# Reordering one DMA queue in every second step of an attention loop: two halves of a move around a send, and a fetch behind them

## The chip, the cores and the metric

The kernel runs on one core of one Trainium2 chip. The metric is device time in microseconds (us) of one execution. The kernel before took 906.04 us as the median of three runs (905.31 to 906.72 us). Everything is in 32-bit floating point.

## The reference

Two layers work on `x` of 16 x 256 x 256 (4096 tokens of 256 channels). Each does `x = x + s * silu(f)`, with `s` and `f` computed from a layer norm of `x`. In layer 0, `s` is a linear recurrence and `f` a two-layer perceptron. Layer 1, where the change is, has causal attention with 16 heads for `s` and a base projection with a routed low-rank part for `f`:

```python
q = (x @ Wq).reshape(B, S, N_HEADS, QK_DIM)                     # 128 plain + 64 rotated
q = jnp.concatenate([q_nope, apply_rope(q_rope)], axis=-1)
k = jnp.concatenate([k_nope, jnp.broadcast_to(k_rope, ...)], axis=-1)
scores = jnp.einsum('bqhd,bkhd->bhqk', q, k) * scale            # causal mask, S = 256
attn = jax.nn.softmax(scores, axis=-1)
out = jnp.einsum('bhqk,bkhd->bqhd', attn, v).reshape(B, S, N_HEADS * V_DIM) @ Wo
```

## The kernel before, in words

Layer 1 works through 8 chunks of 512 tokens (two batch rows of 256). In each chunk the 16 heads form 4 **groups** of 4 heads, so there are 32 groups, numbered n = 0 to 31. Each group takes two **slots** of the loop at L1653, one for each batch row b: slot i = 2n is the even slot of group n (b = 0), slot 2n + 1 its odd slot (b = 1). The whole order is written out by hand: each engine, and the DMA queue of SP (`sp`), is wrapped in `InOrder` (L45), which keeps its instructions in the order in which the loop calls them. The 64 slots run from about 266 us to 880 us of the span.

What one group needs, in order of time:

- `query_mm`, `query_mul`, `query_rot` (L389 to L428): TensorE projects the queries into `pq`; VectorE multiplies by the rotation tables; GpSimd forms the rotated queries `qrot` in two halves, r = 0 and then r = 1, each by one instruction. `qrot` has one buffer.
- `query_move` (L430): the queries must lie in other partitions, so eight DMAs of 64 KB on SP's queue copy `qrot` into the tile `qg`, first four (one for each head) for r = 0, then four for r = 1. Below, **R0** and **R1** are these two sets of four. This is done in the even slot of the group before.
- `score_pack` (L1369): TensorE multiplies `qg` with the keys into `sc`; VectorE adds the mask and takes the row maxima; ScalarE takes the exponential into `pr`; GpSimd normalises (`normalise`, L1405).
- `turn` (L1418): VectorE transposes `pr` in 32 x 32 blocks into `turned`, by three instructions in the slot after the scores.
- `send` (L1430): four DMAs of 192 KB write `turned` to a scratch tile `far` in DRAM. The **S0** send (b = 0) is issued in the group's own odd slot, the **S1** send (b = 1) in the even slot of the next group.
- `fetch` (L1444): four DMAs of 384 KB read `far` back into the tiles `pT`. F(y,b) fetches half y of batch row b: F(0,0) and F(1,0) in the even slot of the next group, F(0,1) and F(1,1) in the odd slot after that. Each waits until the sends of its b have landed.
- `values_of` (L1490): two slots after S1, in the even slot of group n + 2, TensorE multiplies `pT` with the values (`av`). It takes y = 0 first, b = 0 before b = 1, then y = 1.

So SP's queue issues 20 DMAs for each pair of slots. Before the change their order is

- even slot: R0 and R1 of group n + 1, F(0,0) of group n - 1, S1 of group n - 1, F(1,0) of group n - 1;
- odd slot: F(0,1) and F(1,1) of group n - 1, S0 of group n.

In the program as built, the DMAs of SP take eight completion semaphores in turn, and each waits for the landing of the one eight places ahead of it; at most eight are under way. SP waits in order: while one DMA waits, nothing behind it in the queue is issued.

Of the kernel before, what the change touches and what calls it, by code (L numbers as in the profile page):

```python
# [41 lines left out]
def tile_two_layers(ctx: ExitStack, tc: tile.TileContext, d: dict, out: bass.AP):  # L42
# [384 lines left out]
        gp.tensor_tensor(q.rot[:, 0, :], m0[:, 0, :], m1_[:, 1, :], ALU.subtract)  # L427
        gp.tensor_tensor(q.rot[:, 1, :], m1_[:, 0, :], m0[:, 1, :], ALU.add)  # L428

    def query_move(n):  # L430
        q = groups[n]
        for r in range(2):
            for h in range(G):
                sp.dma_start(
                    q.qg[64 + 32 * r : 96 + 32 * r, :, h, :],
                    q.rot[32 * h : 32 * h + 32, r, :].rearrange("p (a q) -> p a q", q=32),
                )


    with ExitStack() as l0:  # L440
# [177 lines left out]
        for k in range(8):  # L618
            n = 1 << k
# [714 lines left out]
    def gate_end(ch, jp):  # L1334
        k = chunks[ch]
        g = k.g2[:, 2 * jp : 2 * jp + 2, :]
        ve.scalar_tensor_tensor(g, g, 1.0, k.h, ALU.add, ALU.mult)
# [31 lines left out]
    def score_pack(u, pi):  # L1369
        k, b, pack = chunks[u.ch], u.b, PACK[pi]  # L1370
        if pi == 0:
            u.nm = sm1.tile([P, NQ], F32, tag="nm", name=f"nm_{u.n}", bufs=3)
            u.sr = sm1.tile([P, NQ], F32, tag="sr", name=f"sr_{u.n}", bufs=3)
        qg = groups[u.i // 2].qg
        sc = ps_sc.tile([P, CH], F32, tag="sc", name=f"sc_{u.n}_{pi}")
        halves = 2 if pi == 2 and u.b == 0 and u.i > 4 else 1
        m = P // halves
        for a, o in pack:
            w = qg[:, b * NQ + a, :, :].rearrange("p h q -> p (h q)")
            for y in range(halves):  # L1380
                pe.matmul(
                    sc[m * y : m * y + m, o : o + 32 * (a + 1)], w[:, m * y : m * y + m],
                    k.kT[:, b * S : b * S + 32 * (a + 1)], start=True, stop=True,
                )
        ends = [o + 32 * (a + 1) for a, o in pack]
        step = ends[1] - ends[0]
        n = len(pack)
        assert ends == [ends[0] + step * z for z in range(n)]
        if ends[0] - 32 + step * n <= CH:
            diag = sc[:, ends[0] - 32 : ends[0] - 32 + step * n].rearrange("p (n s) -> p n s", n=n)[:, :, 0:32]  # L1390
        else:
            diag = sc[:, ends[0] - step : ends[-1]].rearrange("p (n s) -> p n s", n=n)[:, :, step - 32 : step]
        ve.tensor_tensor(diag, diag, bc(kmask, n), ALU.add)
        for a, o in pack:
            ve.tensor_reduce(
                u.nm[:, a : a + 1], sc[:, o : o + 32 * (a + 1)], AX.X, ALU.max, negate=True
            )
        for a, o in pack:
            w = 32 * (a + 1)
            ac.activation(  # L1400
                u.pr[:, OFF[a] : OFF[a] + w], sc[:, o : o + w], AF.Exp,
                bias=u.nm[:, a : a + 1], accum_out=u.sr[:, a : a + 1],
            )

    def normalise(u, packs):  # L1405
        blocks = [a for pi in packs for a, _ in PACK[pi]]
        lo, hi = min(blocks), max(blocks) + 1
        ve.reciprocal(u.sr[:, lo:hi], u.sr[:, lo:hi])
        for a in blocks:
            v = u.pr[:, OFF[a] : OFF[a] + 32 * (a + 1)]  # L1410
            gp.tensor_scalar(v, v, u.sr[:, a : a + 1], 1.0, ALU.mult, ALU.mult)
# [32 lines left out]
    def fetch(n, y, b):  # L1444

        q = groups[n]
        if y == b == 0:
            q.pT = {}
        if b == 0:
            q.pT[y] = pp.tile([P, G, 3 * P], F32, tag="pT", name=f"pT_{n}_{y}", bufs=3)  # L1450
        sp.dma_start(
            q.pT[y][64 * b : 64 * b + 64].rearrange("p h q -> p (h q)"),
            q.far[b].rearrange("(y k) s h z q -> y (k s) (h z q)", y=2)[y],
        )
# [82 lines left out]
    def out_weights(i):  # L1537
        if i == PER:
            gp.tensor_tensor(TO[1], wo(0, 1), wo(0, 0), ALU.subtract)
            gp.tensor_tensor(TO[2], wo(1, 1), TO[1], ALU.subtract)  # L1540
        elif i == PER + 2:
            gp.tensor_tensor(TO[4], TO[2], wo(1, 0), ALU.subtract)
        elif i == PER + 4:
            gp.tensor_tensor(TO[3], wo(1, 1), wo(0, 1), ALU.subtract)
        elif i == 2 * PER + 1:
            TO[4] = X[0].rearrange("p j (n s) -> p (j n) s", s=DH)[:, 0:KP]
            gp.tensor_tensor(TO[4], TO[2], wo(1, 0), ALU.subtract)
# [45 lines left out]
    def fast_begin(ch, r):  # L1593

        k = chunks[ch]
        if r == 4:
            fast_sum(ch, (1, 1), (0, 1), (1, 1), ALU.add)
            fast_sum(ch, (0, 1), (0, 0), (0, 1), ALU.subtract)
        elif r == 5:
            fast_sum(ch, (0, 0), (1, 1), (0, 0), ALU.subtract)  # L1600
            fast_out(ch, 0, k.c00, (0,))
        elif r == 6:
            fast_sum(ch, (1, 0), (1, 0), (0, 0), ALU.subtract)
            k.c1 = a2.tile([P, 2, D], F32, tag="h", name=f"c1_{ch}", bufs=1)
            gp.tensor_tensor(k.c1[:, :, 0:DH], k.v, k.p4, ALU.subtract)
            gp.tensor_tensor(k.c1[:, :, DH:D], k.v, k.p5, ALU.add)
            gp.tensor_tensor(k.u, k.u, k.p5, ALU.add)
        elif r == 7:
            fast_out(ch, 1, k.c1, (0, 1))
            fast_store(ch, 1)  # L1610
        elif r == 0:
            fast_out(ch, 0, k.c01, (1,))
            fast_store(ch, 0)
# [39 lines left out]
    for i in range(LAST):  # L1653
        ch, r = divmod(i, PER)
        odd = i % 2 == 1
        u, w = units[i], units[i - 1] if i else None
        here = w is not None and w.i >= LAST - 2
        n = (i + 3) // 2 if odd else (i + 2) // 2
        n = n if n < len(groups) else None
        more = ch + 1 < NCH  # L1660
        last = ch - 1 if ch == NCH - 1 and r in FINISH else None
        fast = ch - 1 if 0 < ch < NCH - 1 else None

        if not odd and n is not None:
            query_move(n)
        if odd and i > 2:
            fetch((i - 3) // 2, 0, 1)
            fetch((i - 3) // 2, 1, 1)
        elif i and not odd:
            fetch((i - 2) // 2, 0, 0)  # L1670
        score_pack(u, 0)
        if w:
            normalise(w, (2,))
        if fast is not None and r > 3:
            fast_begin(fast, r)
        if ch > 1 and r == 0:
            fast_begin(ch - 2, 0)
        out_weights(i)
        if r == 1:
            gate_end(ch, 0)  # L1680
        if r == 2:
            gate_end(ch, 1)
            if more and ch:
                norm_end(ch + 1)
        if r == 5 and more:
            kv_end(ch + 1)
        if i == LAST - 1:

            finish_mm(last, 3, 0, NPAIR)
            finish_out(last, 3)  # L1690
            last = None
        if w:
            for z in (1, 2):
                turn_here(w, z) if here else turn(w, z)

        if r == 0:
            mid_chunk(ch)
        if r == 7 and more:
            key_chunk(ch + 1)
        if n is not None:  # L1700
            query_mm(n, 0 if odd else 3)
            if not odd:
                query_lat(n, 3)
        if i == 5:
            values_of(0)
        score_pack(u, 1)

        if odd and n is not None:
            query_mm(n, 1)
            query_mul(n, 0)  # L1710
        if w:
            if here:
                turn_here(w, 0)
            else:
                turn(w, 0)
                send(w)
        if not odd:
            if i > 4:
                values_of((i - 4) // 2)
            if i:  # L1720
                fetch((i - 2) // 2, 1, 0)
        score_pack(u, 2)
        normalise(u, (0, 1))

        if odd and n is not None:
            query_mm(n, 2)
            query_mul(n, 1)
            query_rot(n)
            query_lat(n, 2)
        if r < 2:  # L1730
            gate_begin(ch, r)
        if r == 0 and more and ch:
            norm_begin(ch + 1)
        if r == 2 and more:
            transpose_chunk(ch + 1)
        if r == 4 and more:
            kv_begin(ch + 1)
        if r == 6 and more:
            router_chunk(ch + 1)
        if last is not None:  # L1740
            j = FINISH.index(r)
            finish_mm(last, j, 0, NPAIR)
            finish_out(last, j)
        if fast is not None and r in FINISH:
            fast_end(fast, r)
# [94 lines left out]
```

## Time and profile before

| | |
|---|---|
| median of the runs | 906.04 us |
| profiled execution, its own time | 903.67 us |
| span of the profiled execution | 901.9 us |
| granted TensorE clock, mean | 0.994 |
| TensorE busy (PE) | 889.3 us, 99% of the span |
| VectorE, ScalarE, GpSimd busy | 667.4, 476.0, 571.2 us |
| DMA queue of SP | 128.69 MB, 58.0% of the span of 16 engines |
| from 300 to 857 us | PE busy 553.93 of 557.00 us, DMA share 0.81 |

The profiled execution took 1.77 us more than its span, and 2.37 us less than the median of the runs. In the profile's lines the file line of nearly all instructions is that of the wrapper, L53, so groups are told apart by their tiles: `far<-turned` is a send, `pT<-far` a fetch, `qg<-qrot` a move, `av<-pT,rowv` the matmuls of `values_of`. "SPq" is SP's queue; the duration of one of its rows runs from the first to the last issue that it merges. A fetch takes 4.0, 4.9 and 6.3 us from issue to landing (least, median, most), a send 2.3, 4.4 and 6.6 us, a move 2.1, 2.7 and 5.9 us.

### The profile page before, as it was taken

Reading aid. Unit: us, or ns where it says so; the run is one execution under the profiler, and the core shown is the slowest. Engines: PE = TensorE matmul, PEld = TensorE weight load, DVE = VectorE, ACT = ScalarE, POOL = GpSimd, SP = SyncE. Lnnn points to the kernel's source line nnn. Section 1 sums busy time; section 2 is a strip of 40 time slices with the busy share of each in tenths; the row PEclk is TensorE's granted clock in tenths of the full one; section 3 lists DMA queues with packets and bytes.
Section 4 is the critical chain, followed back from the end, with each engine's and each line's share of the span. In section 5 each row is a group of like instructions: output and inputs, shape, how many; then the busy total and the mean of one; then the engine's idle time right before and its main releaser. Section 6 shows DMA issues by size and latency. Waiting matters only on the chain.

```text
span 901.9 us, 17976 instructions
## 1 busy us (share of the span) xinstructions
PE 889.3 (99%) x5688; PEld 666.8 (74%) x5688; DVE 667.4 (74%) x2017; ACT 476.0 (53%) x1562; POOL 571.2 (63%) x885
## 2 busy tenths in 40 slices
PE   9999999999999989999999999999999999999988
PEld 8777999987757657776776777677677767766766
DVE  6886678764687869678868867886886788687642
ACT  3234665644436646655655565565556556556441
POOL 2229687787355537787586677758667775876531
PEclk9999999999999999999999999999999999999989
DMA  9730000000024888887887887788788768878880
GB/s 276 245 118 1 1 2 1 1 1 1 1 32 79 230 209 198 186 207 161 217 218 169 206 181 201 180 217 214 170 200 211 190 170 209 210 176 194 209 223 29
DMA packets 197406, 134.04 MB, mean 149 GB/s; under 512 B 143104, under 2 KB 187968, under 8 KB 197312
## 3 DMA queue, kind: packets, MB, share of 16 engines
q1 hardware_dynamic: 195184, 128.69, 58.0%
q0 software_dynamic: 1152, 3.67, 1.2%
q8 instruction: 46, 0.75, 0.4%
q10 hardware_dynamic: 976, 0.53, 0.2%
q14 instruction: 48, 0.39, 0.1%
HBM read 63.11 MB, written 52.95 MB: 129 GB/s over the span
## 4 chain that ended last, share of the span: by engine, by line
PE 93%; DVE 3%; DMA 2%; POOL 1%; ACT 1%; SPq 0%; issue 0%; ACTq 0%; POOLq 0%
PE pq L53 23%; PE sc L53 14%; PE po L53 11%; PE av L53 8%; PE f L53 7%; PE r L53 7%; PE pg L53 5%; PE ph L53 5%; PE pf L53 5%; PE pm L53 2%; PE pkv L53 2%; PE tp L53 2%; DMA far<-turned 1%; DMA pT<-far 1%; PE pb L53 1%; PE py L53 1%
## 5 line engine op out<-in xcount | busy, mean ns | idle before, releaser
L53 POOL TENSOR_SCALAR pr<-pr,sr 128x256 f32<-128x256 f32 (+7 forms) x512 | 192.5, 397 | 188.2 <-DVE sr L53 180.3
L53 ACT ACTIVATE pr<-sc,nm 128x256 f32<-128x256 f32 (+7 forms) x512 | 190.2, 382 | 217.1 <-DVE sr L53 139.6
L53 PEld LDWEIGHTS sc<-kT,qg 128*128 128x128 f32 (+1 forms) x1198 | 150.8, 176 | 54.8 <-issue 41.6
L53 PE MATMUL sc<-kT,qg 128*128 128x32 f32 (+6 forms) x1198 | 169.0, 290 | 0.0
L53 DVE TENSOR_REDUCE nm<-sc 128x1 f32<-128x256 f32 (+7 forms) x512 | 127.5, 301 | 6.6
L53 DVE STREAM_TRANSPOSE turned<-pr 128x512 f32<-128x512 f32 x186 | 123.2, 687 | 11.0 <-POOL pr L53 10.9
L53 PE MATMUL pq<-xnT,wlat 128*128 128x512 f32 x256 | 122.7, 602 | 0.0
L53 PE MATMUL pq<-xnT,wrope 128*128 128x512 f32 x256 | 120.2, 593 | 0.0
L53 ACT ACTIVATION_READ_ACCUMULATOR pr<-sc,nm 128x1 f32 x512 | 104.0, 203 | 0.0
L53 PE MATMUL av<-pT,rowv 64*64 64x512 f32 (+2 forms) x992 | 80.5, 445 | 6.0 <-DMA pT<-far 6.0
L53 POOL TENSOR_TENSOR qrot<-qmul,qmul 128x512 f32<-128x512 f32 x64 | 83.6, 1329 | 2.8 <-DVE qmul L53 2.8
L53 DVE TENSOR_TENSOR sc<-sc,kmask 128x96 f32<-128x96 f32 (+1 forms) x192 | 45.2, 236 | 53.8 <-PE sc L53 52.5
L53 DVE TENSOR_TENSOR qmul<-pq,rot_q 128x512 f32<-128x512 f32 x128 | 80.7, 672 | 0.1
L53 ACT ACTIVATE qg<-pq 64x512 f32<-64x512 f32 x128 | 75.5, 590 | 4.3 <-PE pq L53 3.5
L53 PEld LDWEIGHTS av<-pT,rowv 64*64 64x64 f32 x992 | 39.8, 135 | 43.6 <-issue 30.1
L53 PEld LDWEIGHTS pq<-xnT,wrope 128*128 128x128 f32 x256 | 45.7, 191 | 32.4 <-issue 32.1
L53 PEld LDWEIGHTS pq<-xnT,wlat 128*128 128x128 f32 x256 | 45.7, 191 | 31.6 <-issue 31.6
L53 PEld LDWEIGHTS po<-wout,attT 128*128 128x128 f32 x416 | 59.3, 193 | 9.8 <-issue 3.5
L53 PE MATMUL po<-wout,attT 128*128 128x128 f32 (+1 forms) x416 | 65.3, 311 | 0.0
L53 POOL TENSOR_TENSOR attT<-attT,attT 128x512 f32<-128x512 f32 x36 | 45.1, 1273 | 0.0
L53 POOL TENSOR_TENSOR rs<-ve,mhalf 128x4 f32<-128x4 f32 (+1 forms) x17 | 16.8, 987 | 41.1 <-DVE ve L53 33.6
L53 PE MATMUL pf<-p2T,hT 128*128 128x256 f32 x192 | 42.7, 380 | 0.0
(229 smaller groups left out, 1520.0 us busy)
## 6 DMA issues: line engine op xcount, KB each, us to landing
far<-turned SPq DMA_DIRECT2D x248, 192.0 KB, 4.4
pT<-far SPq DMA_DIRECT2D x124, 384.0 KB, 4.9
qg<-qrot SPq DMA_DIRECT2D x256, 64.0 KB, 2.7
x<-in_x_dram SPq DMA_DIRECT2D x7, 512.0 KB, 10.4
out_dram<-x POOLq DMA_DIRECT2D x12, 256.0 KB, 4.0
wqn_wo<-in_wq_nopeT_dram SPq DMA_DIRECT2D x4, 512.0 KB, 5.4
wqn_wo<-in_Wo_dram SPq DMA_DIRECT2D x4, 512.0 KB, 6.8
p2T<-in_proj2T_dram SPq DMA_DIRECT2D x2, 512.0 KB, 8.3
```

The source lines that it names most:

```text
L53: r = getattr(self.engine, name)(*args, **kw)
```

## The change

In the even slot, `query_move` is called twice, once for each half r, and the fetch F(0,0) is called later. The new order of SP's queue in an even slot is: R0, S1, R1, F(0,0), F(1,0). The odd slot is as it was. All 20 DMAs of a pair of slots stay, with the same sizes, and no other engine's instructions change in kind, number or order.

```diff
-    def query_move(n):
+    def query_move(n, part=(0, 1)):
         q = groups[n]
-        for r in range(2):
+        for r in part:
             for h in range(G):
                 sp.dma_start(
                     q.qg[64 + 32 * r : 96 + 32 * r, :, h, :],
...
-        if not odd and n is not None:
-            query_move(n)
         if odd and i > 2:
             fetch((i - 3) // 2, 0, 1)
             fetch((i - 3) // 2, 1, 1)
-        elif i and not odd:
-            fetch((i - 2) // 2, 0, 0)
+        if not odd and n is not None:
+            query_move(n, (0,))
         score_pack(u, 0)
...
                 turn(w, 0)
                 send(w)
         if not odd:
+            if n is not None:
+                query_move(n, (1,))
+            if i:
+                fetch((i - 2) // 2, 0, 0)
             if i > 4:
                 values_of((i - 4) // 2)
             if i:
                 fetch((i - 2) // 2, 1, 0)
```

## Prediction

> **What bounds the kernel now.** I read the page first: the busy shares, then the chain that ended last. After that I read the chain in order of time around its DMA pieces, TensorE's timeline at those places, and SP's queue there and in an undisturbed pair of slots.
>
> ```profile
> PE 889.3 (99%) x5688; PEld 666.8 (74%) x5688; DVE 667.4 (74%) x2017; ACT 476.0 (53%) x1562; POOL 571.2 (63%) x885
> PE 93%; DVE 3%; DMA 2%; POOL 1%; ACT 1%; SPq 0%; issue 0%; ACTq 0%; POOLq 0%
> ```
>
> TensorE is the bound, and no change of a queue takes matmuls away. What a queue can give is in the rest of the chain: DMA has 2%, some 18 us, and it lies in two places:
>
> ```profile
> 310.10 5.26 DMA far<-turned
> ...
> 315.50 4.27 DMA pT<-far
> ...
> 319.91 3.70 PE av L53 x20
> ```
>
> ```profile
> 854.38 4.83 DMA far<-turned
> ...
> 859.36 0.45 SPq L53
> 859.81 0.05 issue
> 859.86 5.58 DMA pT<-far
> 865.44 0.04 issue
> 865.48 1.97 PE av L53 x10
> ```
>
> In both, TensorE waits for the last two fetches, which waited for the S1 send. TensorE's timeline gives the prices:
>
> ```profile
> 315.77 1.08 PE L53 MATMUL av<-pT,rowv 64*64 64x512 f32 x4
> 319.91 3.70 PE L53 MATMUL av<-pT,rowv 64*64 64x512 f32 x28 [3.07 <-DMA pT<-far]
> ...
> 859.95 1.07 PE L53 MATMUL av<-pT,rowv 64*64 64x512 f32 x4
> 863.81 1.51 PE L53 MATMUL av<-pT,rowv 64*64 64x512 f32 x16 [2.78 <-DMA pT<-far]
> 865.48 1.97 PE L53 MATMUL av<-pT,rowv 64*64 64x384 f32 x12 [0.17 <-DMA pT<-far]
> ```
>
> An undisturbed `values_of` takes 2.38 us (at 304.99). Here group 1 takes 315.77 to 323.61, 7.84 us, and group 29 takes 859.95 to 867.45, 7.50 us: 5.46 and 5.12 us lost, more than the idle figures say, because matmuls that wait are drawn long. Five other groups lose a little in the same timeline: 2.75 us at 337.78, 2.83 at 435.60, 2.67 at 592.80, 2.84 at 749.76 and 2.64 at 845.83, together 1.83 us over 2.38. So at most 5.46 + 5.12 + 1.83 = 12.4 us can be won from fetches. Elsewhere from 300 to 857 us PE is busy for 553.93 of 557.00 us.
>
> Why are those fetches late? SP's queue in the pair of slots of group 1's wait, and in that of group 29's:
>
> ```profile
> 301.78 5.94 SPq L53 DMA_DIRECT2D qg<-qrot  x8
> 307.76 0.63 SPq L53 DMA_DIRECT2D pT<-far  x1
> 308.49 2.65 SPq L53 DMA_DIRECT2D far<-turned  x4
> 311.24 5.36 SPq L53 DMA_DIRECT2D pT<-far  x3
> ```
>
> VectorE ended the last transpose that S1 needs at 303.59 (302.88 + 0.71). The send starts at 308.49: it stood 4.9 us behind eight moves and one fetch. In the even slot of group 29's send the transpose ended at 847.64 and the send starts at 852.80, 5.2 us later. The chain names a VectorE instruction on the output as what let that send go; I don't believe it, since the queue reached the send only then. SP's own waits list 81.9 us (65 times) for `far<-turned`: after F(1,0) the queue stands idle until S1 has landed.
>
> **The change part by part.**
>
> *S1 goes ahead of R1 and F(0,0).* Four moves at 628 ns with 0.04 between them are 2.7 us and the fetch 0.7, so S1 is issued up to 3.4 us earlier, where its transpose is done. Where it isn't, S1 goes when it is.
>
> *R1 goes behind S1.* S1 needs a wait for VectorE, which R1 and the four fetches now queue behind; R1 is wanted by the first `sc` matmul of the next pair, and by GpSimd before it may overwrite `qrot`. In the undisturbed pair R1 is issued from 516.9 and has landed about 522; after the change S1 goes at 518.91 (transpose), takes 2.6, and R1 lands about 2.7 behind its own 2.7 of issue, or behind S1's landing: 526.9 to 528. The next `sc` is at 529.25 in TensorE's timeline and GpSimd's next `qrot` at 528.7. That is a cover of about 1 to 2 us; it costs nothing while it holds. It is thinnest for group 2: S1 goes at 289.7 (end of the transpose at 289.04), R1 at 292.3 to 295.0, landing at 297 to 298 against an `sc` at 296.56. TensorE would wait 0 to 1.5 us, but 19 us before a wait for `pT` that stays in part (next paragraph) and is timed by SP, not by TensorE; I add nothing for it.
>
> *F(0,0) goes behind both.* It is only needed with the others, since `av` needs all of b = 0 and b = 1 for each y. But now four fetches of 384 KB are issued in a row. The row for how they share the DMA engines is group 29's: issued at 859.36 and 859.86 by the chain, landed at 863.81 and 865.48 by TensorE's starts: 4.45 us for the first, and 1.67 us more for the one behind it. So with the burst beginning at time T, F(0,1) lands at T + 4.45 + 2 x 1.67 = T + 7.8, F(1,1) at T + 9.5, if the burst is what limits it; if only S1's landing limits, F(0,1) is issued when S1 has landed and takes 4.45.
>
> *Group 1.* R0 starts at 301.78, half of 5.94 is 2.97: S1 goes at 304.8, ends its issue at 307.4; R1 ends at 310.4 = T. F(0,1) lands at 318.2, against 319.91 now: 1.7 us won at least. With S1's landing as the limit (last send 306.8 + 5.26 = 312.1, fetch + 4.45 = 316.5) it is 3.4 us. R0 can also start up to 1 us earlier (`qrot` was ready at 300.7). I take 2.5 of the 5.46, between the two.
>
> *Group 29.* If nothing before it were earlier: R0 at 844.13 + half of 7.90 = 848.1, S1 to 850.9, R1 to 854.8 = T; F(0,1) at 862.6, 1.2 us won. But the pair before is earlier too: its transpose ended at 830.59 and its send started at 834.89, so its fetches come some 3 us sooner; the moves then start at 842.4 (`qrot`) and are not held up by earlier DMAs (8 at 0.67 are 5.4 us, not 7.90). R0 to 845.1, S1 at 847.64 to 850.4, R1 to 853.1 = T: F(0,1) at 860.9, 2.9 us won; by S1's landing alone it would be all 5.1. I take 3.3.
>
> *The five small losses* sum to 1.83; each pair's S1 is 1 to 4 us earlier, and I take 1.4.
>
> Once a wait for `pT` is gone, the next thing late is TensorE's own work; VectorE and GpSimd stood idle in these waits (VectorE 4.0 us before 324.17, 4.7 us before 868.39, both for `sc`), so they don't take it back.
>
> The sum, against the profiled execution: 2.5 + 3.3 + 1.4 = 7.2 us, 903.67 - 7.2 = 896.5 us. The median of the runs stands 2.37 us above that execution, so 906.04 - 7.2 = 898.8 us.
>
> [...]
>
> **The rivals.**
>
> *Half of it (0.20).* One of the two long waits stays, because the four fetches in a row or the DMAs ahead eat the lead. For: T + 9.5 is not far from now in both. Against: the rows of the pair before group 29. Gain 2.5 to 4, time 902.0 to 903.7.
>
> *No change (0.10).* The burst takes what the earlier send gives: with 2.3 us a fetch F(0,1) lands at T + 9.1, which is 319.5 for group 1. The wait then moves from S1's landing to the DMA engines. Time 904.5 to 907.
>
> *Slower (0.12).* R1 lands too late. The send's wait stands ahead of it in every even slot, and the price falls on `sc` at the head of the next pair. It decides from the point where R1 lands over 2 us later than I reckon, as with a send at its longest, 6.6 us instead of 4.4, and a move's issue at its longest, 2.0 us instead of 0.63. If it holds in one pair of four (8 of 31), at 2 us each, it costs 16 us and takes back the 7.2: 914.8. For it: a cover of 1 to 2 us in the undisturbed pair. Against it: S1 and R1 have no fetch ahead of them any more.
>
> That the change doesn't do what it says is no rival: the queue is in written order.
>
> **How the numbers follow.** The forecast has 0.58, with its own range of 893.5 (nearly all of the 12.4 us) to 902. A measurement of this kernel can tell about 0.2%, 1.8 us, from no change: faster means under 904.2, slower over 907.9. Faster takes the forecast and the half, 0.78; same 0.10; slower 0.12. The range holds the forecast, the half and some of the unchanged: 893.5 to 905.0.
>
> **What would show it.** Right: in the chain, the DMA pieces near 310 and 854 shrink or go; TensorE's idle time for `pT` at `av` falls from 3.07 and 2.78 us; S1 starts within 0.5 us of its transpose or of R0's end; SP's waits for `far<-turned` fall well below 81.9 us. Wrong: TensorE idle ahead of `sc<-kT,qg` for `qg<-qrot`, GpSimd's `qrot` waiting for moves, or fetches that land more than 6.3 us after issue with `av` waiting as long as now.

## The result, and the profile after

The changed kernel is 0.4% slower: 908.72 us as the median of 14 runs (904.73 to 912.74), against 904.78 us for the kernel before (14 runs, 903.03 to 907.10). The ratio is 1.0042, with a 95% interval of 1.0024 to 1.006. The forecast was 898.8 us and the range 893.5 to 905.0.

Four lines of the page after, its busy shares, its chain and the groups of the score and the values matmuls (busy, mean ns of one, idle before):

```profile
PE 896.5 (99%) x5688; PEld 670.6 (74%) x5688; DVE 667.5 (73%) x2017; ACT 476.6 (52%) x1562; POOL 571.4 (63%) x885
PE 94%; DMA 2%; DVE 2%; SPq 1%; POOL 0%; ACT 0%; issue 0%; POOLq 0%; ACTq 0%
L53 PE MATMUL sc<-kT,qg 128*128 128x32 f32 (+6 forms) x1198 | 169.7, 291 | 0.8 <-DMA qg<-qrot 0.8
L53 PE MATMUL av<-pT,rowv 64*64 64x512 f32 (+2 forms) x992 | 85.4, 445 | 4.6 <-DMA pT<-far 4.5
```

TensorE's count of matmuls is the same, and it is "busy" 7.2 us longer (896.5 against 889.3). The values matmuls take 85.4 + 4.6 = 90.0 us, against 80.5 + 6.0 = 86.5 before: their idle time fell and their busy time rose, because a matmul that waits is drawn long (group 8, below: 3.27 us instead of 2.38, with no idle time).

The chain in order of time, at the wait of group 1:

```profile
312.93 0.18 SPq L53
...
313.80 8.10 DMA pT<-far
321.90 0.04 issue
321.95 1.97 PE av L53 x10
```

The send is gone from the chain, as forecast. In its place one fetch takes 8.10 us (the last one, F(1,1)); before, it was 5.26 us of send and 4.27 of fetch. At group 29 it is the same: one fetch of 7.24 us ends at 870.72. TensorE's timeline after (start, duration, engine, what; idle time in brackets):

```profile
313.57 1.05 PE L53 MATMUL sc<-kT,qg 128*128 128x256 f32 x4 [0.66 <-DMA qg<-qrot]
317.09 1.07 PE L53 MATMUL av<-pT,rowv 64*64 64x512 f32 x4
320.37 3.54 PE L53 MATMUL av<-pT,rowv 64*64 64x512 f32 x28 [2.21 <-DMA pT<-far]
...
457.82 3.27 PE L53 MATMUL av<-pT,rowv 64*64 64x512 f32 x32
...
867.37 1.07 PE L53 MATMUL av<-pT,rowv 64*64 64x512 f32 x4
870.76 3.88 PE L53 MATMUL av<-pT,rowv 64*64 64x512 f32 x28 [2.31 <-DMA pT<-far]
```

The two long waits shrank by less than 1 us each (3.07 to 2.21, 2.78 to 2.31). A wait for R1 at `sc` is new. And an ordinary group, number 8 at 457.82, now takes 3.27 us, where 2.38 is undisturbed; it had no wait before.

SP's queue in an ordinary pair shows why. First the kernel before, then the changed one; the same pair, 4.4 us later in the second:

```profile
513.31 6.97 SPq L53 DMA_DIRECT2D qg<-qrot  x8
520.33 0.63 SPq L53 DMA_DIRECT2D pT<-far  x1
521.06 2.56 SPq L53 DMA_DIRECT2D far<-turned  x4
523.72 4.41 SPq L53 DMA_DIRECT2D pT<-far  x3
```

```profile
517.74 3.70 SPq L53 DMA_DIRECT2D qg<-qrot  x4
523.38 2.86 SPq L53 DMA_DIRECT2D far<-turned  x4
526.34 3.00 SPq L53 DMA_DIRECT2D qg<-qrot  x4
529.38 2.55 SPq L53 DMA_DIRECT2D pT<-far  x4
```

The transposes ended at 518.91 and at 523.35. Counted from there, the send starts after 2.15 us before and 0.03 us after: the change does what it says. But the last two fetches are issued 8.1 and 8.6 us behind the transpose before (527.04, 527.54), and 7.4 and 8.0 after, although SP need no longer wait for the send; R1's issue stands there instead. And they land later: the four fetches of the second listing, all issued within 2.55 us, take 4.6, 5.8, 6.9 and 8.1 us to land, in their order, where the last two took 4.3 and 5.6 before. On the mean of groups 2 to 27 (worked out from the trace: landing of F(1,1) less the end of the transpose that its send needs), the last fetch lands 15.3 us behind the transpose before, and 16.5 after. The median fetch takes 6.5 us, against 4.9.

### The profile page after: what moved, and what is told of

Read it like the earlier page. It is cut to its first block, busy times and chain, and to the rows that moved or that the text cites. A ratio compares the mean times of both kernels' runs of the same rounds, so it can differ in the third digit from the quotient of the medians.

```text
span 908.6 us, 17799 instructions
## 1 busy us (share of the span) xinstructions
PE 896.5 (99%) x5688; PEld 670.6 (74%) x5688; DVE 667.5 (73%) x2017; ACT 476.6 (52%) x1562; POOL 571.4 (63%) x885
## 4 chain that ended last, share of the span: by engine, by line
PE 94%; DMA 2%; DVE 2%; SPq 1%; POOL 0%; ACT 0%; issue 0%; POOLq 0%; ACTq 0%
PE pq L53 24%; PE sc L53 15%; PE po L53 10%; PE av L53 9%; PE f L53 7%; PE r L53 7%; PE pg L53 5%; PE ph L53 5%; PE pf L53 5%; PE pm L53 2%; PE pkv L53 2%; DMA pT<-far 2%; PE tp L53 2%; PE pb L53 1%; PE py L53 1%; SPq L53 1%
## 5 line engine op out<-in xcount | busy, mean ns | idle before, releaser
L53 PE MATMUL av<-pT,rowv 64*64 64x512 f32 (+2 forms) x992 | 85.4, 445 | 4.6 <-DMA pT<-far 4.5
L53 PEld LDWEIGHTS av<-pT,rowv 64*64 64x64 f32 x992 | 42.0, 134 | 44.8 <-issue 24.8
```

What stands on the lines that cost most here:

```text
L53: r = getattr(self.engine, name)(*args, **kw)
```

## The experiments

Orders are those of SP's queue in the even slot. The change is R0, S1, R1, F(0,0), F(1,0). Theory A: the loss comes from the row of four fetches behind R1. Theory B: from R1 being late. Theory C, from the page's clock row, is on the two long waits: in the profile before, the clock is at half for 3.41 us from 319.22 us, at the end of the one wait, and for 6.83 us from 865.35, behind the other. Each ratio is to the kernel before, run in the same session (medians of 904.68 to 905.80 us).

**Undo the late fetch.**

```diff
         if not odd and n is not None:
             query_move(n, (0,))
+        if i and not odd:
+            fetch((i - 2) // 2, 0, 0)
...
                 query_move(n, (1,))
-            if i:
-                fetch((i - 2) // 2, 0, 0)
```

> Even slot in the order R0, F(0,0), S1, R1, F(1,0): the change with its late fetch undone. Theory A (four fetches in a row): the last fetch lands late because F(0,0) stands directly ahead of the three others; with it back ahead of S1, TensorE's small waits at av (groups 3, 4, 7, 8, 11, 12, 15, 16, 20, 23, 24, 27 in the changed kernel, 0.3 to 0.9 us each) go away, and S1 is still some 2.7 us earlier than in the kernel before: 899 to 903 us. Theory B (R1 behind the send is what costs): R1 is as late as in the change, so it stays at 907 us or more, with TensorE waiting for qg<-qrot. The median fetch takes about 5 us to land by A, 6.5 us by B.

Measured: 898.79 us, ratio 0.9926 (0.9904 to 0.9948). That this is the forecast's 898.8 is chance: it is another order. R1 has the same place as in the change and lands 8.6 us behind the transpose on the mean (8.3 in the change), and still the kernel is 10 us faster than it, so B is not the cause. The median fetch takes 5.4 us; the values matmuls:

```profile
L53 PE MATMUL av<-pT,rowv 64*64 64x512 f32 (+2 forms) x992 | 79.1, 437 | 2.2 <-DMA pT<-far 2.1
```

**The late fetch alone**: `query_move(n)` whole ahead of S1, F(0,0) behind S1.

> Even slot in the order R0, R1, S1, F(0,0), F(1,0): the late fetch alone, the moves whole and ahead of the send as before. Theory A: the four fetches in a row are there and S1 is only 0.7 us earlier than before, so it is at least as slow as the change: 908 to 912 us, median fetch 6 us or more. Theory B: R1 is early again, so it is like the kernel before, 904 to 906 us.

Measured: 905.03 us, ratio 0.9998 (0.998 to 1.0016). This is a miss for theory A as I had put it: in the median, the late fetch alone costs nothing. (The profiled execution took 908.71 us, the longest of its 12, so its trace lies above the median.) The median fetch takes 6.1 us here, but the row begins sooner, right behind S1, and its last fetch lands 15.2 us behind the transpose, as before. The row is not as dense either: F(0,1) must wait for S1's landing, and the four issues of the ordinary pair take 3.89 us, where they take 2.55 in the change.

```profile
523.38 2.46 SPq L53 DMA_DIRECT2D far<-turned  x4
525.88 3.89 SPq L53 DMA_DIRECT2D pT<-far  x4
```

It is the two together, R1 between the send and the row of fetches, that makes the last landing late. This is theory A1 below.

**R1 last of all**: R0, F(0,0), S1, F(1,0), R1.

> Even slot in the order R0, F(0,0), S1, F(1,0), R1: R1 goes to the place where SP's queue stood idle for the landing of S1. Theory A: the fetches are spread as before and S1 is 2.7 us earlier: 898 to 902 us. Theory B: R1 is later still, TensorE waits for it at sc in most pairs: 909 us or more, and GpSimd's qrot waits for moves.

Measured: 902.27 us, ratio 0.996 (0.9944 to 0.9977), just over A's range. Both mechanisms show: the waits for fetches are gone, and waits for R1 have come.

```profile
L53 PE MATMUL sc<-kT,qg 128*128 128x32 f32 (+6 forms) x1198 | 169.2, 290 | 7.5 <-ACT qg L53 4.0 <-DMA qg<-qrot 1.7 <-DVE qmul L53 1.4
L53 PE MATMUL av<-pT,rowv 64*64 64x512 f32 (+2 forms) x992 | 75.0, 436 | 0.3 <-DMA pT<-far 0.3
```

Where the first line names another engine the wait is R1's too: in each of these places the last move lands 0.1 to 0.3 us before the matmul. So R1 can be too late, 10.5 us behind the transpose on the mean, but at the change's 8.3 it costs 0.8 us.

**F(0,0) and R1 exchanged**: R0, S1, F(0,0), R1, F(1,0).

```diff
-            if n is not None:
-                query_move(n, (1,))
             if i:
                 fetch((i - 2) // 2, 0, 0)
+            if n is not None:
+                query_move(n, (1,))
```

> Even slot in the order R0, S1, F(0,0), R1, F(1,0): the change with F(0,0) and R1 exchanged. Theory A1 (it takes both: the fetches in a row, and R1's issue of 2.7 us between the send and the first of them): the fetches start right behind the send, the last one lands 1.2 to 1.5 us earlier than in the change, and the time is like that of the split alone, 897 to 901 us. Theory A2 (any fetch behind the send is late, whatever stands between): like the change, 906 to 910 us. In the changed kernel, seen from the end of the transpose, the last fetch lands after 16.5 us on the mean of groups 2 to 27, in the kernel before after 15.3 us.

Measured: 896.6 us, ratio 0.9911 (0.989 to 0.9932), the fastest of all and just under A1's range. F(0,0) is behind the send as in the change; all that differs is that it is issued ahead of R1. A1 holds, A2 falls. The queue, and the last fetch 15.2 us behind the transpose on the mean:

```profile
518.45 2.42 SPq L53 DMA_DIRECT2D far<-turned  x4
520.92 0.62 SPq L53 DMA_DIRECT2D pT<-far  x1
521.64 2.92 SPq L53 DMA_DIRECT2D qg<-qrot  x4
524.66 2.26 SPq L53 DMA_DIRECT2D pT<-far  x3
```

The page's groups show what it wins and what it pays:

```profile
L53 PE MATMUL sc<-kT,qg 128*128 128x32 f32 (+6 forms) x1198 | 168.3, 289 | 2.7 <-DMA qg<-qrot 2.7
L53 PE MATMUL av<-pT,rowv 64*64 64x512 f32 (+2 forms) x992 | 76.7, 436 | 0.1
```

**Two doses.** In one kernel F(0,0) is cut into two halves, one ahead of S1 and one behind R1. In the other, two of R1's four moves stand ahead of F(0,0) and two behind it.

> The change with F(0,0) cut in two: the first two heads' half of its bytes ahead of S1, as in the split alone, the other half behind R1, as in the change. Theory A (what lies in the row of fetches behind R1 sets the last landing): a dose between the split alone (898.8) and the change (908.7): 901 to 906 us, and the last fetch lands 15.6 to 16.2 us behind the transpose. Rival (only the first fetch's place counts, or the number of DMAs): equal to one of the two ends, within 1 us.

> The change with only half of R1 (two of its four moves) between the send and F(0,0), the other half behind F(0,0). Theory A1 (R1's time of issue ahead of the row of fetches counts): a dose between the order with F(0,0) first (896.6) and the change (908.7): 899 to 905 us. Rival (what counts is whether R1 is whole or that F(0,0) directly follows the send): equal to one of the two ends, within 1 us.

Measured: 901.98 us (0.9961, 0.9943 to 0.998) and 899.84 us (0.9939, 0.9922 to 0.9955). Both lie between their ends. So does the last landing behind the transpose: 15.6 us for the half fetch (15.2 for the split alone, 16.5 for the change) and 15.8 us for half of R1 (15.2 with F(0,0) first). The ratios' intervals lie clear of the change's and overlap a little with those of the faster ends.

The last landing in the ordinary pairs is not all of the time, though: the kernel before and the two fastest orders have the same 15.2 to 15.3 us. The traces give the rest (one profiled execution each, in us: the last landing behind the transpose on the mean of groups 2 to 27, then the sums of the times from the first start to the last end of `values_of`):

| order | last landing | groups 1 and 29 | the other 29 groups |
|---|---|---|---|
| kernel before | 15.3 | 15.3 | 71.1 |
| the change | 16.5 | 14.1 | 75.9 |
| late fetch undone | 15.2 | 9.3 | 72.0 |
| late fetch alone | 15.2 | 15.8 | 73.3 |
| R1 last of all | 14.0 | 4.8 | 70.5 |
| F(0,0) ahead of R1 | 15.2 | 6.0 | 70.9 |
| half of F(0,0) early | 15.6 | 10.4 | 72.1 |
| half of R1 between | 15.8 | 6.9 | 72.5 |

The change loses in the 29 groups; what the faster orders win over the kernel before lies in groups 1 and 29, and in the clock behind them (a mean of 1.000 and 0.998 in the profiles of the split alone and of F(0,0) ahead of R1, 0.994 in that of the kernel before). Part of that win has only moved: in the orders of 4.8, 6.0 and 6.9 us, TensorE waits 2.5 to 3.1 us for R1 at `sc` near 300 us, ahead of group 1.

**The long waits filled.** Extra matmuls, whose result the next matmul overwrites, go ahead of `values_of` in chosen groups. First, the kernel before:

```diff
-NWARM = 16
+NWARM, FILL = 16, {1: 5, 29: 5}
...
         av = [m1(f"av_{ch}_{g}_{b}", [P, 2, S]) for b in range(2)]
+        for _ in range(FILL.get(n, 0)):
+            pe.matmul(
+                av[0].rearrange("p a s -> p (a s)"), wlat[:, 0, 0:2, :],
+                chunks[ch].xnT[:, 0, :], start=True, stop=True,
+            )
```

> The kernel before, with five extra 128x128x512 matmuls (about 4.3 us of TensorE work, their result overwritten) ahead of the values matmuls of groups 1 and 29, in the two places where TensorE waited about 3 us. Theory C (the granted clock falls to half for 3.4 or 6.8 us after each of these waits): the extra work lies in time that was lost anyway and the clock stays at 1.00, so the kernel gets faster by 2 to 5 us, 900 to 903 us, and the granted clock's mean is 0.998 or more. Rival (the halved clock has nothing to do with the wait, or costs nothing): 904 to 907 us, with the clock at half in the same places.

Measured: 900.6 us, ratio 0.995 (0.9932 to 0.9969): more work and less time. The stage view around group 1's wait (stretch; its length; busy times of PE, PEld, DVE, ACT, POOL; then the granted clock), first before, then filled:

```profile
315.00:319.00 4.00, 1.84 (x11) 0.84 (x9) 3.19 (x11) 3.72 (x11) 4.00 (x7) 1.00 0.65 150
319.00:323.00 4.00, 3.09 (x24) 1.70 (x26) 0.71 (x1) 0.59 (x4) 0.41 (x2) 0.57 1.02 282
```

```profile
315.00:319.00 4.00, 4.00 (x15) 2.09 (x14) 3.05 (x10) 3.71 (x13) 4.00 (x8) 1.00 0.50 125
319.00:323.00 4.00, 4.00 (x35) 1.69 (x33) 0.71 (x1) 0.45 (x5) 0.27 (x2) 1.00 0.95 273
```

Before, TensorE stands still until about 319.9 and is granted 0.57 of its clock in the stretch from 319 us, with 3.41 us of it at half (from 319.22); filled, it keeps 1.00.

> The kernel before, with the five extra matmuls ahead of the values matmuls of groups 5 and 13 instead, where the fetches had landed some 6 us before. Theory C: there they only cost: 2 x 4.3 us, 912 to 916 us, and the two halved clocks stay. Rival (the filler helps for another reason, such as the order in the memory of TensorE): under 907 us.

Measured: 910.99 us, ratio 1.0069 (1.0047 to 1.009). Where there is no wait the same work costs 6.0 us over the 904.98 of the kernel before in that session, less than the 8.6 us of the expectation; the clock's mean stays at 0.994 in every run. Why it doesn't cost all of it was not tried.

**The change with its long waits filled.**

> The change as it is, with five extra 128x128x512 matmuls ahead of the values matmuls of groups 1 and 29. Theory C with theory A: the two long waits and their halved clock go, 4 to 6 us, and what stays are the small waits in the other groups, which the kernel before does not have: 902 to 905 us, 2 to 4 us over the same filler in the kernel before (900.6). Rival (the long waits are all of the difference): equal to that, 900 to 901 us.

> The change with the filler of five matmuls in groups 1 and 29, and with both halves of the move first in slots 2 and 4. It takes out the two waits for R1 (0.16 and 1.25 us at sc). Theory A: what is left over the filled kernel before (900.6 us) are small waits at av: 905 to 906 us, 1 to 1.5 us less than the filled change (906.92). Theory B (R1 late is most of the loss): 901 to 903 us.

Measured: 906.92 us (1.0024, 1.0012 to 1.0035), and with both halves of the move first in slots 2 and 4, 906.15 us (1.0022, 1.0006 to 1.0037). In all runs of the first the clock's mean is 1.00. So the long waits and the halved clock are not what makes the change slower than the kernel before: without them it is still 6.3 us over the filled kernel before, more than the 2 to 4 expected. The two profiled executions have spans of 905.1 and 900.9 us; of these 4.2 us, the values matmuls are 81.4 + 0.6 against 79.3, 2.7 us, and the waits for R1 1.4 us. With R1 early in slots 2 and 4 no wait at `sc` is left, and the time falls by 0.8 us only, just over theory A's 905 to 906: R1's lateness is not most of the loss.

**A better version yet.** The split with its remaining waits filled, and the fastest order with the move whole in slot 2:

> Even slot in the order R0, F(0,0), S1, R1, F(1,0), with 2, 3 and 1 extra matmuls ahead of the values matmuls of groups 1, 29 and 30 (their result is overwritten). Theory C: the rest of the waits is filled, the clock stays at 1.00 in every run, and the slowest runs of the split order (over 899 us, with the clock's mean at 0.996) go: median 896 to 898 us. Rival: the filler is just work, 900 to 902 us.

> The order R0, S1, F(0,0), R1, F(1,0) everywhere but in slot 2, where both halves of the move go first, as in the kernel before. In the fastest order so far TensorE waits 2.54 us at sc for group 2's R1 (at 299.4 us) and runs at half clock for 3.41 us behind it. If that wait is R1's and the half clock is the wait's, both go: 2.5 + 1.7 us less than 896.6, but the wait for group 1's fetches may come back in part: 892 to 895.5 us. Rival (the wait only moves to av of group 1, which was timed by SP): 896 to 898 us.

Measured: 898.33 us (0.9931, 0.9912 to 0.9951) and 897.31 us (0.9925, 0.9909 to 0.9941); neither beats 896.6, and in the split the filler is worth nothing clear of noise (898.79 without it). The second went as its rival had it: the wait for R1 at 299.4 us is gone, and two others have come: 2.07 us at `sc` of the next pair (314.62), and values matmuls of 2.68 us in group 1 instead of 2.38.

## Why the prediction was wrong

**What was right.** The bound and the two waits; that S1 would go at the end of its transpose (0.03 us behind it in the ordinary pair); that SP's waits for `far<-turned` would fall, from 81.9 to 1.6 us; and the price of the row of fetches: T + 7.8 and T + 9.5 us were put down for the last two landings, and with T = 529.38 they came at about T + 8.3 and T + 10.0. R1 behind S1 cost 0 to 1.5 us at group 2 by the text, and 0.8 us in all by the page.

**The step that failed** is "The five small losses sum to 1.83; each pair's S1 is 1 to 4 us earlier, and I take 1.4". I worked out the row of fetches for the two pairs with a long wait only, and for all others counted the earlier send as an earlier fetch. My own terms, put into the undisturbed pair, say the contrary: S1 at 518.91, its 2.6 us and R1's 2.7 make T = 524.2, so the last fetch lands at 533.7, where before it was issued at 527.54 and landed 5.6 us later, at 533.1. Little was to spare there: before, 10 of the 29 groups other than 1 and 29 begin their values matmuls less than 1 us after F(0,1) has landed, or ahead of it (group 12 itself has 1.4 us: landed at 531.3, begun at 532.7). So the 1.4 us to be won became a loss: the values matmuls of these 29 groups take 75.9 us instead of 71.1, 4.8 us more, and the page's group rose by 3.5 us although the two long waits shrank. From the forecast (7.2 us less) to the profile (6.7 us more) it is 13.9 us; this term makes 6.2 of them, and groups 1 and 29 make 4.6.

**Groups 1 and 29** were expected to win 2.5 and 3.3 us. In the profile group 1 now takes 317.09 to 323.91, 6.8 us instead of 7.84, and group 29 takes 867.37 to 874.64, 7.3 instead of 7.50. Group 1 has won nothing by it: the transpose ends at 303.6 us in both, S1 lands at 311.39 instead of 315.35, and yet F(0,1) lands at 320.24 instead of 319.77. The wait is shorter because TensorE comes 1.3 us later, and the group ends 0.3 us later than before. In group 29 F(0,1) lands 15.4 us behind the transpose instead of 16.1. Two terms were too small. The four moves of R0 take 4.89 and 5.05 us to issue, where 2.97 and 2.7 were put down: by the eighth place in the queue they wait for the landing of the late fetches ahead of them, 2.1 and 2.6 us here, though the text has those of group 29 "not held up by earlier DMAs" (SP's waits for `pT<-far` in all: none listed before, 29.9 us in 33 places after). In group 29 two of these moves are issued at 851.07 and 852.95 us, each 0.02 us behind the landing of the fetch eight places ahead; of SP's 620 DMAs from 266 to 880 us never more than eight are under way in this trace. And R1's four take 3.09 and 3.79 us instead of 2.97 and 2.7 ahead of the row of fetches.

**The sum after**, in the two profiled executions (spans 908.6 and 901.9 us, 6.7 apart): 3.5 us in the values matmuls, 0.8 at `sc`, and about 1.7 from 3.4 us more at half clock (the stage 322 to 329 us has a clock of 0.52: 6.83 us at half from 321.92, against 3.41 in this place before). 0.7 us is left. The clock's part is not the change's own: at the same mean clock of 0.994 the runs of the change average 909.0 us (5 runs), those of the kernel before 905.0 (9 runs of the first session).

**The rivals.** "No change" named the mechanism, the burst, but let it only take back the gain; its 2.3 us a fetch was an assumption, and in the ordinary pair of the change the four landed 1.8 to 1.9 us apart. "Slower" named another one, R1's lateness, and the runs with R1 in the same place and no loss rule it out as the main cause. F(0,0) issued early makes 898.79 us of the change's 908.72. But the fastest order, 896.6 us, issues F(0,0) behind the send too, and the fetch alone issued late costs nothing in the median (905.03 us); so its place in the queue alone does not tell what it costs.

## What to carry to other kernels

When a queue is reordered, put the price of the new order into a pair of steps that has no wait now, and set it against the time to spare there; there are many such pairs, and few with the wait that the change is after. A transfer that other work waits for has to be early at its landing, not at its issue: in the ordinary pair of the change the last fetch is issued 0.6 us sooner behind the transpose than before, and lands 1.9 us later. If a wait of TensorE of some 3 us can't be removed, filling it with matmuls may pay, as it did in the kernel before (900.6 us, ratio 0.995); where there was no such wait, they were only work (910.99 us, ratio 1.0069).

## What the runs showed of the hardware

Four fetches of 384 KB issued 0.65 us apart landed 4.6, 5.8, 6.9 and 8.1 us after their own issue, some 1.8 us from one landing to the next; spread out as in the kernel before, the median took 4.9 us.

TensorE idle times of 3.07 and 2.78 us in the kernel before went with 3.41 and 6.83 us at half clock, those of 2.21 and 2.31 us in the change with 6.83 us each, and one of 3.09 us at `sc` (R1 last of all, ended at 300.56 us) with a granted clock of 0.83 and 0.74 in the stretches from 298 to 302 and from 302 to 306 us. With those of 0.58 and 1.11 us (in the split alone), 3.1 us in all at `sc` (with half of R1 between) and 2.07 us (in the last experiment), the mean clock of the execution was 1.000. So in these runs the length of the idle time alone does not decide it. The mean clock of 24 runs of the same kernel before ranged from 0.989 to 0.998, and the time with it: 906.9 us on the mean of the four runs at 0.991, 903.2 of the two at 0.998.
